# Gnn-to-gnn units of a four-layer graph network: fetched tiles' scores and the side products placed earlier and pinned, the diagonal's sum formed in the next unit

## The chip, the cores and the metric

The kernel runs on one core of a Trainium2 chip. The time is microseconds on the device for one execution of the whole program; the figure used is the median of several runs. The five engines of the core are TensorE (PE, with its weight loads shown apart as PEld), VectorE (DVE), ScalarE (ACT), GpSimd (POOL) and SyncE (SP), and each works through its own instructions in order. Transfers between the chip's memory and the on-chip buffers are issued by SP and POOL.

## The reference

There are 64 graphs of 256 nodes with 256 features each, all with the same sparse symmetric adjacency matrix. Layers 0, 1 and 3 are alike ("gnn" layers), layer 2 is an attention layer. Everything is in float32.

```python
# layers 0, 1 and 3; h is (64, 256, 256)
pre_u = einsum('bud,dk->buk', h, W1[:d]); pre_v = einsum('bvd,dk->bvk', h, W1[d:])
hidden = relu(pre_u[:, :, None, :] + pre_v[:, None, :, :] + b1)
S = sigmoid(einsum('buvk,ko->buvo', hidden, W2)[..., 0] + b2[0])
a_t = einsum('buv,bud->bvd', S * adj, h)
m_t = einsum('uv,bud->bvd', adj, h) * h
z = beta1*h + beta2*(a_t @ Wa + ba) + beta3*(m_t @ Wm + bm)
# layer 2
feats = data @ W1.T; f1 = feats @ W2 + b2[0]
coefs = softmax(leaky_relu(f1[:, :, None] + f1[:, None, :]) + adj)
out = coefs @ feats + bias2 + data
```

Since S is multiplied by adj, only scores of pairs that are joined by an edge are needed. The kernel computes the scores of edges and of the diagonal alone.

## The kernel before

**Edges as tiles.** The edges are sorted once, at the start, into 16 blocks of up to 128 edges, a few left over ("left", one score column), and the diagonal. One block is a tile of 128 edges for two graphs: a row holds pre_u of the edge's one end plus pre_v (with b1) of the other. Eight blocks (`FAST`) are *made* by PE: a 0/1 matrix `pick` times rows gathered in `pre`, which ACT copies out of pu and pv (rows_u L754, rows_v L763); the product is `ga` (L700). The other eight (`FETCHED`) are *fetched*: pu and pv are written by SP to tables in the chip's memory (L635, "tableu", "tablev"), and POOL gathers rows of them by index (L745), first from the u table, then from the v table with an add onto the first. `FETCHES` is the order of these 18 gathers (16 for tiles, two for `left`, written -1); each gather is kept behind the one before it. The first six are issued when half of the tables is written, the rest at the start of the next unit.

**Scores.** For each tile and graph DVE computes relu, times W2, and the sum over the row in one instruction (`rated`, L664, two per tile by `both`), into a column of `raw`. `rated_all` makes the sigmoid of a stretch of columns: ACT computes `val` (L684, L685), and DVE multiplies it into the edge values (`rm`, L692). The columns come in two stretches. EARLY holds left, the diagonal and the blocks of row half m = 0; LATE holds the blocks of m = 1. Diagonal scores come from `own` = pu + pv of the same node, which `before` adds on DVE from PSUM (L639). `early` puts the left-over edges and the diagonal into the score matrix `sa`: PE computes the `sides` (L774), DVE adds the diagonal (L778). `spread` puts the other edges in: PE multiplies rm by `gu` (L790, first the half m = 0, then m = 1), and DVE adds the result to sa (L792).

**Units.** Graphs go in pairs, in two streams, a and b. A *unit* is one call of `beside(heavy, light)`: `heavy` is the scores of one stream's pair in one layer, `light` is everything else for the other stream's pair, from the end of one layer to the start of the next:

- `after`: spread (L790), then `finish`: aT = h times sa (L281 with sa), the products with Wm and Wa (L369, or L355 after layer 3), and the sum hT on DVE (L372);
- in the unit to layer 2 and on, `attention` (L404 to L454);
- `before`: pu and pv of the next layer in four groups (L628), which ACT and DVE take out of PSUM (L629, L630), the tables, and for layer 1 the two `turn`s (transposes, L287); then `mixed`: the products with adj (L281 with adj), two PSUM tiles whose elementwise product (mT) is kept for the next unit (`later`, L795).

Light is a generator that yields after each piece how many made tiles (`p`) and fetched tiles (`f`) of heavy come next; `got` in `before` gives some of these numbers. A scheduler then orders each engine's instructions by priority and its own costs, so an instruction may stand elsewhere than the program puts it, unless `tc.issue_after` holds it behind another.

Six units make a round of four graphs, and there are 16 rounds: two that go from layer 0 to layer 1 (the *first* and *second gnn unit*), then the first and second attention unit, then two that close layer 3 and open layer 0 of the next graphs (the *layer-3 units*). The scores of a unit are used at the start of the next but are computed beside the other stream, so a late score delays L790 of the next unit. PSUM has five buffers `ps` for light work and three `ga` for made tiles.

Of the kernel before, what the change touches and what calls it, by code (L numbers as in the profile page):

```python
# [15 lines left out]
P = 128  # L16
# [16 lines left out]
FAST = [(0, 0, 2), (0, 0, 3)] + [(0, 1, i) for i in range(4)] + [(1, 0, 2), (1, 0, 3)]  # L33
# [4 lines left out]
FETCHES += [(-1, 0), (2, 1), (4, 0), (3, 1), (5, 0), (-1, 1), (6, 0), (4, 1), (7, 0), (5, 1), (6, 1), (7, 1)]  # L38

AHEAD = 6  # L40

# [16 lines left out]
def quarter(q):  # L58
    return slice(q * 64, (q + 1) * 64)

# [18 lines left out]
def adj_seq_kernel(ctx: ExitStack, tc: tile.TileContext, a: dict, out: bass.AP):  # L79
# [15 lines left out]
    mm = nc.tensor.matmul  # L95
# [36 lines left out]
    def z_weights(l):  # L132
        for kept, n, beta in ((wm, "Wm", "beta3"), (wa, "Wa", "beta2")):
            kept[l] = const.tile([P, 2, D], FP, name=l + n)
            nc.sync.dma_start(out=kept[l], in_=a[l + n].rearrange("(c p) e -> p c e", p=P))
            nc.scalar.mul(kept[l], kept[l], sca(l + beta))
        zbias[l] = const.tile([P, 2], FP, name=l + "zbias")
        zb = const.tile([P, 2], FP, name=l + "zb")
        nc.vector.tensor_scalar(zb, vecs[:, VEC[l + "ba"], :], sca(l + "beta2"), None, ALU.mult)
        nc.vector.scalar_tensor_tensor(  # L140
# [5 lines left out]
    for l in GNN:  # L146
        halfb2[l] = const.tile([P, 1], FP, name=l + "halfb2")
        nc.vector.tensor_scalar(halfb2[l], sca(l + "b2"), 0.5, None, ALU.mult)
    twob2 = const.tile([P, 1], FP, name="twob2")
    nc.vector.tensor_scalar(twob2, sca("L2_gnn_b2"), 2.0, None, ALU.mult)  # L150
# [7 lines left out]
    def counts(keep, pool, pc):  # L158
# [3 lines left out]
        nc.vector.tensor_scalar(mask, adj, 0.0, None, ALU.not_equal)  # L162
# [6 lines left out]
        nc.vector.tensor_tensor_scan(upto.rearrange("p s v -> p (s v)"), flat, flat, 0.0, ALU.add, ALU.bypass)  # L169
        past = pool.tile([P, 8], FP, name="past")  # L170
        nc.vector.memset(past, 0.0)
        nc.vector.tensor_copy(past[:, 1:8], upto[:, 0:7, 63])
        deg = pool.tile([P, 8], FP, name="deg")
        nc.vector.tensor_tensor(deg, upto[:, :, 63], past, ALU.subtract)
# [17 lines left out]
        nc.vector.tensor_copy(first, t[:, 0:8])  # L192
        last = keep.tile([P, 8], FP, name="last")
        nc.vector.tensor_tensor(last, first, deg, ALU.add)

        over = pool.tile([P, 8], FP, name="over")
        nc.vector.tensor_scalar(over, t[:, 8:16], -128.0, 0.0, ALU.add, ALU.max)
        begin = keep.tile([P, 9], FP, name="begin")
        nc.vector.memset(begin, 0.0)
        nc.vector.tensor_tensor_scan(begin[:, 1:9], over, over, 0.0, ALU.add, ALU.bypass)  # L200
        t = pc()
        mm(out=t[:, 0:1], lhsT=other, rhs=begin[:, 8:9], start=True, stop=True)
        nc.vector.tensor_scalar(begin, begin, t[:, 0:1], None, ALU.add)
        number = keep.tile([P, 8, 64], FP, name="number")
        shift = pool.tile([P, 8], FP, name="shift")
        nc.vector.tensor_tensor(shift, first, past, ALU.subtract)
        nc.vector.tensor_tensor(number, upto, shift.unsqueeze(2).to_broadcast([P, 8, 64]), ALU.add)
        nc.vector.tensor_tensor(number, number, mask.rearrange("p m (s v) -> p (m s) v", v=64), ALU.mult)
# [3 lines left out]
    with tc.tile_pool(name="pc", bufs=2, space=bass.MemoryType.PSUM) as pc, tc.tile_pool(name="cnt", bufs=1) as cnt:  # L212
# [3 lines left out]
        nc.vector.tensor_scalar(many, end, float(LEFT), None, ALU.is_gt)  # L216
# [11 lines left out]
    def attention_weights(one, psum):  # L228
# [8 lines left out]
        nc.vector.tensor_copy(w2q[:, :, D], t[:, 0:2])  # L237
        for c in range(2):
            nc.vector.tensor_scalar(qb[:, c, :], ones, w2q[:, c, D : D + 1], None, ALU.mult)

    def last_bias(one):
# [3 lines left out]
        nc.vector.tensor_scalar(zbrow, zbrow, sca(LAST + "beta2"), None, ALU.mult)  # L245
        nc.vector.scalar_tensor_tensor(zbrow, bmrow, sca(LAST + "beta3"), zbrow, ALU.mult, ALU.add)
# [19 lines left out]
    def stages(pools):  # L266
# [16 lines left out]
        def flip(o, src):  # L283

            for m in range(2):
                for c in range(2):
                    nc.tensor.transpose(o[:, m, blk(c)], src[:, c, blk(m)], ident)  # L287
# [22 lines left out]
        def mixed(st, l, later=None):  # L310

            st["mT"] = mT = one.tile([P, 2, 2, N], FP, tag="mT" + st["side"], name="mT")
            for g in range(2):
# [3 lines left out]
                if later is None:  # L317
                    nc.vector.tensor_tensor(*times)
# [4 lines left out]
        def kept(st, l):  # L323

            hb = one.tile([P, 2, 2, N], FP, tag="hb", name="hb")
            for i in range(2):
                if l == LAST:
                    for m in range(2):
                        nc.vector.scalar_tensor_tensor(
                            hb[:, i, m, :], st["h"][i][:, m, :], sca(l + "beta1"), zbrow, ALU.mult, ALU.add  # L330
                        )
                else:
                    nc.scalar.activation(  # L333
# [4 lines left out]
        def finish(st, l):  # L338

            sa, mT = st["sa"], st["mT"]  # L340
            few_scores = l == GNN[1]
            hb = kept(st, l)
            aT = one.tile([P, 2, 2, N], FP, tag="aT", name="aT")
            for g in range(2):
                t = psum()
                product(t, st["h"][g], sa[:, :, g, :])
                nc.scalar.copy(aT[:, :, g, :], t)
                yield 0 if few_scores else 1
            if l == LAST:
                for g in range(2):  # L350
                    z = psum()
                    for m in range(2):
# [4 lines left out]
                        yield m * (1 + g), 1  # L357
                    o = h_tile(st, g)
                    nc.vector.tensor_tensor(o, hb[:, g], z, ALU.add)
# [606 lines left out]
```

## Time and profile before

| | us |
|---|---:|
| runs shown, median (lowest to highest) | 3519.05 (3515.6 to 3520.39) |
| profiled execution, its time | 3512.57 |
| its span, first to last instruction | 3510.1 |
| PE busy in it | 3447.8 |
| DVE / POOL / ACT busy | 2610.0 / 2230.7 / 1598.8 |
| mean granted TensorE clock | 0.993 |

One round, from the timeline of PE (each unit from its first L790 to the next unit's):

| unit | median us over the rounds |
|---|---:|
| first gnn, second gnn | 32.3, 33.05 |
| first attention, second attention | 43.3, 42.55 |
| first layer-3, second layer-3 | 30.9, 31.5 |

The page gives shares of busy time by engine, the span in 40 slices, the chain of waits that ended last, and groups of instructions by line. A float32 matmul shows as two records. A record of PE lasts longer than its share of the engine, since matmuls overlap: for the time that PE needs, read the distance from one start to the next. The waits view lists an engine's idle time by what ended it. A row of a timeline has the start, the time from first start to last end, the engine, line, operation, tiles and number of records, and in brackets the idle time before it with what ended it.

### The profile page before, as it was taken

The numbers are of one execution on the slowest core, as the hardware profiler recorded it, in microseconds if no ns is written. First come the engines' busy times: TensorE is split into PE (matmuls) and PEld (weight loads), VectorE is DVE, ScalarE is ACT, GpSimd is POOL, SyncE is SP. The second block draws the span as 40 slices with busy tenths as digits, with TensorE's granted clock in tenths as the row PEclk, the third lists the DMA queues.
The fourth block names the chain that finished last, engine by engine and source line by source line (L and its number), as shares of the span: only waits on it lengthen the run. The fifth ranks groups of instructions, "written<-read, shape, count | busy, mean of one in ns | idle before, by whom it ended". The sixth has DMA issues, their size and how long they took to land.

```text
span 3510.1 us, 48385 instructions
## 1 busy us (share of the span) xinstructions
PE 3447.8 (98%) x14328; PEld 2108.7 (60%) x14328; DVE 2610.0 (74%) x10584; ACT 1598.8 (46%) x2929; POOL 2230.7 (64%) x1754
## 2 busy tenths in 40 slices
PE   6999999999999999999999999999999999999998
PEld 3566565656656566565666656656565665656655
DVE  5778686777777777777777777768677777777776
ACT  2454444444444444544444444444444444445452
POOL 3757667575666757667576675766757566675764
PEclk7999999999999999999999999999999999999999
DMA  5768777686777868778687786877768687786865
GB/s 149 168 151 189 155 184 165 163 180 153 186 156 174 177 143 193 158 175 182 142 195 158 181 170 155 188 155 185 163 165 178 149 188 154 179 181 148 192 148 114
DMA packets 274733, 587.25 MB, mean 167 GB/s; under 512 B 37024, under 2 KB 54304, under 8 KB 274464
## 3 DMA queue, kind: packets, MB, share of 16 engines
q0 software_dynamic: 190464, 427.93, 61.4%
q1 hardware_dynamic: 82416, 154.96, 12.6%
q8 instruction: 116, 1.90, 0.2%
q10 hardware_dynamic: 1584, 1.20, 0.1%
q14 instruction: 153, 1.25, 0.1%
HBM read 466.51 MB, written 117.44 MB: 166 GB/s over the span
## 4 chain that ended last, share of the span: by engine, by line
PE 67%; DVE 4%; POOL 3%; DMA 3%; issue 2%; ACT 0%; POOLq 0%; DVEq 0%
PE ps L281 13%; PE ga L700 13%; PE ps L628 12%; PE ps L369 8%; PE ps L355 5%; PE ps L790 4%; PE ps L451 3%; PE ps L410 3%; POOL fetched L745 2%; PE ps L287 2%; DMA fetched<-tablev,ids_v 2%; PE ps L774 2%; DVE junk L664 2%; PE ps L404 1%; DVE rm L692 1%
## 5 line engine op out<-in xcount | busy, mean ns | idle before, releaser
L745 POOL DMA_INDIRECT fetched<-tablev,ids_v x768 | 1211.3, 1577 | 351.0 <-issue 237.4
L745 POOL DMA_INDIRECT fetched<-tableu,ids_u x768 | 766.8, 998 | 806.1 <-DMA tableu<-pu 576.1
L700 PE MATMUL ga<-pre,pick 128*128 128x512 f32 x1536 | 775.2, 604 | 10.5 <-DVE junk L664 7.9
L628 PE MATMUL ps<-L_gnn_w,hT 128*128 128x512 f32 x1536 | 695.4, 596 | 5.7 <-DMA hT<-in_xT_dram 5.7
L664 DVE SCALAR_TENSOR_TENSOR junk<-ga,L_gnn_w2row 128x256 f32<-128x256 f32 x1536 | 583.5, 420 | 119.8 <-PE ga L700 114.8
L664 DVE SCALAR_TENSOR_TENSOR junk<-fetched,L_gnn_w2row 128x256 f32<-128x256 f32 x1536 | 596.1, 419 | 32.6 <-DMA fetched<-tablev,ids_v 32.1
L763 ACT COPY pre<-pv 64x512 f32<-64x512 f32 x768 | 473.4, 616 | 107.1 <-DVE pv L630 76.3
L628 PEld LDWEIGHTS ps<-L_gnn_w,hT 128*128 128x128 f32 x1536 | 285.1, 191 | 334.6 <-issue 311.2
L754 ACT COPY pre<-pu 64x1024 f32<-64x1024 f32 x384 | 392.9, 1039 | 3.8
L700 PEld LDWEIGHTS ga<-pre,pick 128*128 128x128 f32 x1536 | 274.9, 191 | 163.6 <-issue 111.9
L372 DVE TENSOR_TENSOR hT<-hb,ps 128x512 f32<-128x512 f32 x128 | 88.0, 688 | 379.0 <-PE ps L369 379.0
L281 PE MATMUL ps<-adj,h 128*128 128x256 f32 x1536 | 361.0, 387 | 6.6 <-DVE own L639 4.7
L281 PE MATMUL ps<-sa,h 128*128 128x256 f32 x1536 | 363.7, 382 | 3.0 <-DVE sa L792 2.6
L281 PEld LDWEIGHTS ps<-sa,h 128*128 128x128 f32 x1536 | 288.9, 190 | 119.3 <-issue 47.3
L629 ACT COPY pu<-ps 128x256 f32<-128x256 f32 x384 | 142.2, 370 | 467.6 <-PE ps L628 449.1
L281 PEld LDWEIGHTS ps<-adj,h 128*128 128x128 f32 x1536 | 284.0, 190 | 77.0 <-issue 34.3
L692 DVE TENSOR_TENSOR rm<-gva,val 128x256 f32<-128x256 f32 x768 | 277.4, 420 | 37.9 <-ACT val L685 27.7
L333 ACT ACTIVATE hb<-hT,L_gnn_zbias,scas 128x512 f32<-128x512 f32 x128 | 97.4, 807 | 450.4 <-DVE hT L372 363.7
L790 PEld LDWEIGHTS ps<-rm,gu 128*64 128x64 f32 x3072 | 175.0, 137 | 123.1 <-PE ps L281 59.1
L369 PE MATMUL ps<-mT,L_gnn_Wm 128*128 128x512 f32 x512 | 240.6, 592 | 0.0
L369 PE MATMUL ps<-aT,L_gnn_Wa 128*128 128x512 f32 x512 | 240.6, 592 | 0.0
L790 PE MATMUL ps<-rm,gu 128*64 128x128 f32 x3072 | 218.5, 280 | 14.6 <-DVE rm L692 12.4
(156 smaller groups left out, 4074.3 us busy)
## 6 DMA issues: line engine op xcount, KB each, us to landing
tableu<-pu SPq DMA_DIRECT2D x192, 256.0 KB
tablev<-pv SPq DMA_DIRECT2D x192, 256.0 KB
hT<-in_xT_dram SPq DMA_DIRECT2D x32, 512.0 KB
h<-in_x_dram SPq DMA_DIRECT2D x64, 256.0 KB
out_dram<-h SPq DMA_DIRECT2D x64, 256.0 KB
fetched<-tableu,ids_u POOLq DMA_INDIRECT x768
fetched<-tablev,ids_v POOLq DMA_INDIRECT x768
L_gnn_w<-in_L_gnn_W_dram SPq DMA_DIRECT2D x6, 256.0 KB
```

The source lines that it names most:

```text
L281: mm(out=o[:, m, :], lhsT=lhs[:, c, blk(m)], rhs=rhs[:, c, :], start=c == 0, stop=c == 1)
L355: mm(out=z[:, m, :], lhsT=y[:, c, g, blk(m)], rhs=w[:, c, :], start=j == 0 and c == 0, stop=j == 1 and c == 1)
L369: mm(out=z, lhsT=w[:, c, blk(m)], rhs=y[:, c], start=j == 0 and c == 0, stop=j == 1 and c == 1)
L628: mm(out=t, lhsT=hT[:, c, g, blk(m)], rhs=w1[l][:, c], start=c == 0, stop=c == 1)
L629: nc.scalar.copy(pu[:, m, g, :], t[:, 0, :])
L664: nc.vector.scalar_tensor_tensor(junk, t, 0.0, w2row[l], ALU.max, ALU.mult, accum_out=raw[:, i : i + 1])
L692: nc.vector.tensor_tensor(rm[:, k, ms, g, :], gva[:, k, ms, :], val[:, i : i + 4].unsqueeze(2).to_broadcast([P, 4, 64]), ALU.mult)
L700: mm(out=t, lhsT=pick[:, k, 4 * m + i, :], rhs=pre[:, n], start=True, stop=True)
L745: this = nc.gpsimd.indirect_dma_start(out=to, out_offset=None, in_=rows, in_offset=bass.IndirectOffsetOnAxis(ap=ids, axis=0), compute_op=( ...
L754: nc.scalar.copy(st["pre"][h, f : f + n], st["pu"][h, m].rearrange("p g d -> p (g d)").unsqueeze(1).to_broadcast([64, n, 2 * D]),)
L763: nc.scalar.copy(st["pre"][halves[1 - k], n], st["pv"][halves[i % 2], i // 2].rearrange("p g d -> p (g d)"))
L790: mm(out=t[h, :, quarter(i)], lhsT=gu[:, k, 4 * m + i, :], rhs=rm[:, k, 4 * m + i], start=True, stop=True)
```

## The change

The units of the two gnn-to-gnn transitions (`placed`) get an order of their own, and some orders change for all units.

- A wrapper (`Noting`) remembers each engine's last instruction. In placed units the made tiles' matmuls, the scores of fetched tiles, left and diagonal, and the first ACT step of `rated_all` are held behind the instruction that the program issued last on that engine (`behind`).
- Light after layer 0 yields fetched tiles from the first piece of `finish` on (`STEPS`), so that EARLY stands ahead of `before`, and `early` is a step of its own ahead of tile 4. EARLY waits for the first four made tiles only; for that `FAST` has the blocks of m = 0 first, and the copies into `pre` follow that order.
- In layer 1, `own` is no longer added in `before`: the unit that computes the scores adds it, from pu and pv, one instruction of 512 columns for each half, and in placed units the diagonal's scores stand ahead of fetched tiles 0 and 1. In the other units they stand with the second and third made tile.
- In `FETCHES` left's v gather goes ahead of tile 5's u gather.

Calls by `nc.vector`, `nc.scalar` and `nc.tensor` become calls by the wrapper everywhere; that is cut here.

```diff
-FAST = [(0, 0, 2), (0, 0, 3)] + [(0, 1, i) for i in range(4)] + [(1, 0, 2), (1, 0, 3)]
+FAST = [(k, 0, i) for k in range(2) for i in (2, 3)] + [(0, 1, i) for i in range(4)]
-FETCHES += [(-1, 0), (2, 1), (4, 0), (3, 1), (5, 0), (-1, 1), (6, 0), ...
+FETCHES += [(-1, 0), (2, 1), (4, 0), (3, 1), (-1, 1), (5, 0), (6, 0), ...
+STEPS = {
+    GNN[0]: [(1, 1), (1, 1), (0, 1), (1, 0), (0, 1), (2, 1)],
+    GNN[1]: [0, 0, 0, 0, 0, 1],
+    LAST: [1, 1, (0, 1), (1, 1), (0, 1), (2, 1)],
+}
+    def behind(engine):
+        return tc.issue_after(engine.last.ins)
...
-                yield 0 if few_scores else 1
+                yield STEPS[l][g]
...
-            got = {LAST: (1, 0, 1, 1), GNN[1]: (1, 1, 1, 1), GNN[0]: (0, 0, 2, 1)}[l]
+            got = {LAST: (1, 0, 1, 1), GNN[1]: (0, 1, 1, 1), GNN[0]: (0, 0, 2, 1)}[l]
-            own = one.tile([P, 2, 2, D], FP, tag="own", name="own")
+            if l != GNN[1]:
+                st["own"] = one.tile([P, 2, 2, D], FP, tag="own", name="own")
...
-                nc.vector.tensor_tensor(own[:, m, g, :], t[:, 0, :], pv[:, m, g, :], ALU.add)
+                if l != GNN[1]:
+                    vector.tensor_tensor(st["own"][:, m, g, :], t[:, 0, :], pv[:, m, g, :], ALU.add)
...
-                    rows_v(st, 2 - 2 * m, 2, 0)
+                    rows_v(st, 4 - 4 * m, 2, 0)
...
                     st["turn"](0)
-                    yield 1
+                    yield 0, 1
                     st["turn"](1)
-                    yield 0, 1
+                    yield 0
...
-        def scores(st, l):
+        def scores(st, l, placed):
+            stay = behind if placed else lambda engine: nullcontext()
...
+                with stay(scalar):
+                    scalar.activation(val[:, cols], raw[:, cols], AF.Tanh, bias=halfb2[l], scale=0.5)
...
+            def itself(m):
+                with stay(vector):
+                    if l == GNN[1]:
+                        vector.tensor_tensor(*(flat(t)[:, m] for t in (own, st["pu"], st["pv"])), ALU.add)
+                    both(own[:, m], DIAGONAL + 2 * m, DIAGONAL + 2 * m + 1)
...
+                    with stay(tensor):
+                        mm(out=t, lhsT=pick[:, k, 4 * m + i, :], rhs=pre[:, n], start=True, stop=True)
...
-                            rows_u(st, 2 * n + 2, 2, n // 2, 1 - n // 2)
-                            if n:
-                                rows_v(st, 2 * n + 2, 2, n // 2)
-                    if n < 2:
-                        both(own[:, n], DIAGONAL + 2 * n, DIAGONAL + 2 * n + 1)
+                            rows_u(st, 2 * n + 2, 2, *FAST[2 * n + 2][:2])
+                            if n != 1:
+                                rows_v(st, 2 * n + 2, 2, FAST[2 * n + 2][0])
+                    if n in (1, 2) and not placed:
+                        itself(n - 1)
...
                     if f == FIRST:
-                        for _ in made:
-                            yield
-                        rated(left, REST)
+                        if placed:
+                            while len(count) < 4:
+                                next(made)
+                        else:
+                            for _ in made:
+                                yield
+                        with stay(vector):
+                            rated(left, REST)
                         rated_all(EARLY, 0)
                         yield
-                    tile_scores(fetched[f], *block)
-                    if f == FIRST + 1:
+                        if placed:
+                            early(st)
+                            yield
+                    if f < 2 and placed:
+                        itself(f)
+                    with stay(vector):
+                        tile_scores(fetched[f], *block)
+                    if f == FIRST + 1 and not placed:
                         early(st)
                     yield
...
-                yield [after(st, GNN[0]), before(st, GNN[1])], (st, GNN[1])
+                yield [after(st, GNN[0]), before(st, GNN[1])], (st, GNN[1]), True
```

## The prediction

> **What bounds the kernel now.** I read the engine shares first, then who TensorE (PE) waits for, then the timeline of PE and VectorE (DVE) across a unit that goes from layer 0 to layer 1.
>
> ```profile
> PE 3447.8 (98%) x14328; PEld 2108.7 (60%) x14328; DVE 2610.0 (74%) x10584; ACT 1598.8 (46%) x2929; POOL 2230.7 (64%) x1754
> ...
> PEclk7999999999999999999999999999999999999999
> ```
>
> PE is busy nearly all the time at full clock, so it sets the time. Busy is not yet packed, though: 512-column records last 592 to 604 ns each in the groups, but in the chain of waits sixteen L369 records take 6.87 us, 429 ns apiece. I therefore count spacing between starts, not busy time. Where nothing waits, 512 columns cost 0.43 us and 256 columns 0.216. Judged so, only some tens of microseconds are waits. PE's waits:
>
> ```profile
> PE ps L790 <- DVE rm L692: 12.4, 10, 6.0
> PE ga L700 <- DVE junk L664: 7.9, 3, 6.8
> ...
> PE ps L281 <- DVE own L639: 4.7, 5, 2.4
> ```
>
> The L700 wait is start-up. The first and third lie in the units of this change. PE where one gnn unit meets the next, then where it meets an attention unit, then where the first gnn unit begins:
>
> ```profile
> 2056.05 1.02 PE L700 MATMUL ga<-pre,pick 128*128 128x512 f32 x2
> 2057.00 1.09 PE L790 MATMUL ps<-rm,gu 128*64 128x128 f32 x16
> 2058.81 1.42 PE L790 MATMUL ps<-rm,gu 128*64 128x128 f32 x16 [0.71 <-DVE rm L692]
> ...
> 2090.07 2.42 PE L790 MATMUL ps<-rm,gu 128*64 128x128 f32 x32
> ```
> ```profile
> 2024.84 1.09 PE L790 MATMUL ps<-rm,gu 128*64 128x128 f32 x16
> 2025.86 1.12 PE L700 MATMUL ga<-pre,pick 128*128 128x512 f32 x2
> 2026.91 1.09 PE L790 MATMUL ps<-rm,gu 128*64 128x128 f32 x16
> 2027.94 1.12 PE L700 MATMUL ga<-pre,pick 128*128 128x512 f32 x2
> ```
>
> The 32 spread records (L790) take 1.70 us from first to last start where nothing waits (the second attention unit, all 16 rounds). In the second gnn unit they take 2.96, in the first attention unit 2.15; the first gnn unit hides its wait behind one L700. What is late is rm, DVE's product of the late scores:
>
> ```profile
> 2051.30 0.43 DVE L664 SCALAR_TENSOR_TENSOR junk<-fetched,L_gnn_w2row 128x256 f32<-128x256 f32 x1 [1.20 <-DMA fetched<-tablev,ids_v]
> ...
> 2051.65 1.46 DVE L692 TENSOR_TENSOR rm<-gva,val 128x256 f32<-128x256 f32 x4
> 2053.03 0.74 DVE L630 TENSOR_TENSOR pv<-ps,L_gnn_b1row 128x256 f32<-128x256 f32 x2
> 2053.69 0.74 DVE L639 TENSOR_TENSOR own<-ps,pv 128x256 f32<-128x256 f32 x2
> 2054.35 1.64 DVE L778 SCALAR_TENSOR_TENSOR sa<-diag,val,ps 128x256 f32<-128x256 f32 x4
> ...
> 2057.66 1.43 DVE L692 TENSOR_TENSOR rm<-gva,val 128x256 f32<-128x256 f32 x4 [0.63 <-ACT val L685]
> ```
>
> The last gather lands at about 2053.2, but 4.3 us of other DVE work stands between 2051.65 and the last three scores, which end near 2057.0; then val, and rm only at 2057.66. Order on DVE, not data, makes it late.
>
> **What the Trainium skill says.** "Perfetto Trace Analysis", Identifying the Most-Contended Engine: matmul busy share is no measure of headroom because matmuls are pipelined. The trace agrees (592 against 429 ns). The same page, DMA Instruction — SWDGE (GPSIMD): a gather's slice ends when its descriptors are written, and the data move later. The trace agrees: a v gather is 1.55 us on POOL, and the one issued at 2045.39 is 5.81 us of DMA in the chain; so I reckon a v gather as landing some 5.2 us after its issue. The same page, Optimization Strategy: the same gap repeating on the engine that should be saturated can mean too few buffers for the next tile. That fits the L281 waits on own, which hold a PSUM buffer, but not L790, whose data are missing.
>
> **The change, part by part.** S is the start of L790 in a gnn unit; the order comes from the built program, durations from rows of before.
>
> 1. *Second gnn unit, late scores.* In the new order DVE does the early rm (1.4) and sa (1.6) before tile 4, and own is not there. For the first gnn unit: the second L628 pair ends at S+28.2, its pu copy (0.37) and pv (0.42) bring DVE to S+29.1; tiles 6 and 7 landed at S+26.4 and 28.4; four scores at 0.345 end at S+30.5; val takes 0.6; rm starts at S+31.2. PE's second half started 1.15 us after rm in the excerpt (2058.81 less 2057.66), so at S+32.35 it is free to run, and PE reaches it near S+33.5. The wait goes, with 1.1 us spare: 2.96 - 1.70 = 1.26 in ten of 16 rounds, 0 to 0.82 in the others: **-15.6 us**.
> 2. *First attention unit.* The same in the second gnn unit, with 0.5 us spare because its gathers start later (5 below): 2.15 - 1.70 = 0.45 in 15 rounds and 1.26 in one: **-8.1**. The small waits of sa,h on sa just after it: -1.2.
> 3. *own out of `before` in layer 1.* The adds that free PSUM late go: L281's waits on own by spacing of starts, **-6.7** (idle alone 4.7). DVE does 64 adds of 512 (0.684, L795's row) for 128 of 256 (0.419): 10 us less, all beside PE, worth nothing further.
> 4. *Pinned L700.* In the first gnn unit L790 becomes one block; L700 no longer stands between its halves. Changes L700 to L790 fall from 126 to 110. A split costs 0.34 (4.06 us against 3.72 for the same records), but it covered a wait: the late rm of the layer-3 unit before starts at 2025.21, S+0.37, and that unit keeps its order. The second half can start at S+0.37+1.15 = 1.52, the block takes 2.67, and with the usual 2.02 to the first sa,h this is 4.69 against 4.06: +0.63 in 16 rounds, **+10.1**.
> 5. *Moved steps and their queues.* One L700 more stands ahead of the first L628 pair (+0.86 after +0.63, less waits gone), so pu reaches SP's table DMA about 1.3 us later; POOL, which already waited 2.8 us for it at 2051.64, starts the next unit's 18 gathers so much later. These take 29 us of 32: they land in time, but half the slack of step 2 goes. On POOL `left`'s v gather goes before one u gather (0.98 plus 0.3): left lands 1.3 us sooner, and the u gather 1.9 later with 4 us in hand. No DMA is added.
> 6. *Waits behind pinned scores.* hT (L372) now stands on DVE behind tiles 1, 2 and 3. Tile 3 lands at S+14.4, and hT's second half is not fed by PE until S+17.5. val stands on ACT ahead of the pu copies; it is ready near S+20, and the first L628 group ends at S+20.9. sides take two of five PSUM buffers early; sa frees them by S+25.6, L628 needs one at S+26.5. All zero while gathers land within 2 us of today's times; 1 us per us beyond.
> 7. L774 sooner: PE changes shape as often as before; zero. FAST order, ACT's copies: the same number, and the rows for the third L700 are ready at S+2.5 for its use at S+3.7; zero. Units not placed: own's scores one L700 later, with none behind them waiting; zero. Start and end of the run: 2 us either way.
>
> The trace doesn't show PE in the pinned order. From below, step 4 may cost nothing (rm a little earlier, the split saved: -5.4); from above, a gather later by its own spread (1 us) takes back steps 1 and 2 in part. I take the values above.
>
> Sum: -15.6 - 8.1 - 1.2 - 6.7 + 10.1 = **-21.5 us**. The profiled execution took 3512.57 us with a span of 3510.1; the median of runs is 3519.05, 6.5 longer, and I take the difference over unchanged: 3519.05 - 21.5 = 3497.5.
>
> **Rivals.** (a) *The gathers become the bound.* Step 5's later table eats the slack, the first attention unit keeps its 0.45 or gets 1 us, and step 1 comes back by half: +8 and -8 for -15.6, net about -4 with steps 3 and 4: 3515, no change. For it: DMA is 81% busy in the gnn units and POOL's sequence fills 29 of 32 us. Against it: tile 7 lands over 4 us ahead of its use. (b) *Slower:* DVE blocks on a gather in front of hT (L372) in the second gnn unit. Slack there is 2.0 us (tile 3 at S+14.75, needed by S+16.75, since PE comes sooner). Beyond that L628 waits us for us; all of the gain is lost when tile 3 is 3.4 us later than today in each round (1.4 times 16), and 4 us give +10: 3529. Against it: nine gathers in ten land within 1 us of the median. (c) *It doesn't place as said:* the built order shows that it does; but if the second gnn unit's stall has another cause (tile 7 itself), steps 1 and 2 are void: +10.1 - 6.7 = 3522.
>
> **How the numbers follow.** 0.2%, about what a measurement here can tell from no change, is 7 us. The sum's case (-8 to -33): 0.77, and more by a free step 4 and fewer stray stalls: 0.04; (a) 0.06 and (c) 0.03, both no change; (b) 0.10. Faster 0.81, same 0.09, slower 0.10. The likeliest case alone spans 3486 to 3511; for eight in ten I reach to part of (a): 3484 to 3514.
>
> **What would show it.** Right: the 32 L790 records of the second gnn and first attention units take about 1.7 us, rm in PE's waits moves to the first gnn unit (near 2.7 us there, some 0.6 to 1 us per round), own vanishes from L281's waits, own<-ps,pv falls to 256 and DVE's busy time by some 10 us. Wrong: L628 or L774 waiting for hT, ro or pu; DVE's waits on fetched ahead of hT; a first gnn unit over 33 us.

## The result, and the profile after

| | us |
|---|---:|
| after, median of 5 runs (lowest to highest) | 3497.66 (3496.77 to 3504.9) |
| before, median of 5 runs beside it | 3519.05 (3515.6 to 3520.84) |
| ratio, 95% interval | 0.9947 (0.9933 to 0.9962) |
| profiled execution after, its time; its span | 3497.66; 3496.0 |

The forecast was 3497.5. Between the two profiled executions the change is smaller, 14.9 us (3512.57 to 3497.66). Run again later, beside other runs of the kernel before, the same changed kernel stood at 0.991 (0.9896 to 0.9925). So the forecast's total hit the first measurement and is small for the second; what separates the two is taken up below.

The wrapper issues nearly everything in the changed kernel, so its profile gives the wrapper's line, L76; rows are told apart by tiles (ps<-rm,gu is L790, ga<-pre,pick L700, ps<-adj,h and ps<-sa,h the two kinds of L281, junk<-fetched the gathered scores). The engine shares:

```profile
PE 3430.6 (98%) x14328; PEld 2112.8 (60%) x14328; DVE 2621.2 (75%) x10520; ACT 1617.1 (46%) x2929; POOL 2244.3 (64%) x1754
```

PE is busy 17.2 us less for the same instructions; DVE is busy 11.2 us more with 64 instructions fewer. TensorE's part of the waits view (us in total, times, longest):

```profile
PE ps L76 <- DVE rm L76: 17.4, 18, 6.3
...
PE ps L76 <- DVE sa L76: 7.3, 8, 1.9
...
PE ps L76 <- DVE own L76: 0.6, 1, 0.6
```

The wait on own is down to one, outside the rounds. The wait on rm is longer than before (17.4 for 12.4; the longest single wait of each, 6.3 and 6.0, is in the run's last unit; the prediction read all 12.4 as lying in the units of the change, but summed by distances of starts). PE's timeline shows where a first gnn unit begins, and then where the second begins:

```profile
2010.51 1.02 PE L76 MATMUL ga<-pre,pick 128*128 128x512 f32 x2
2011.46 1.09 PE L76 MATMUL ps<-rm,gu 128*64 128x128 f32 x16
2014.04 1.42 PE L76 MATMUL ps<-rm,gu 128*64 128x128 f32 x16 [1.49 <-DVE rm L76]
...
2044.23 1.02 PE L76 MATMUL ga<-pre,pick 128*128 128x512 f32 x2
2045.18 1.97 PE L76 MATMUL ps<-rm,gu 128*64 128x128 f32 x32
2047.08 1.98 PE L76 MATMUL ga<-pre,pick 128*128 128x512 f32 x4
```

In the second gnn unit the 32 records are now one piece without a wait, in all 16 rounds. In the first they break after 16, with nothing between: the wait on rm has moved there. (This round is one of two in which a gather came late too: its 32 records take 3.73 us, where the median is 2.70.) DVE's timeline on the way to that second gnn unit:

```profile
2036.52 1.66 DVE L76 SCALAR_TENSOR_TENSOR sa<-diag,val,ps 128x256 f32<-128x256 f32 x4 [0.23 <-PE ps L76]
...
2041.38 0.42 DVE L76 TENSOR_TENSOR pv<-ps,L_gnn_b1row 128x256 f32<-128x256 f32 x1 [0.61 <-ACT pu L76]
2041.73 0.41 DVE L76 SCALAR_TENSOR_TENSOR junk<-fetched,L_gnn_w2row 128x256 f32<-128x256 f32 x1
...
2043.84 1.43 DVE L76 TENSOR_TENSOR rm<-gva,val 128x256 f32<-128x256 f32 x4 [0.63 <-issue]
```

sa is done before the late scores, and only four scores stand between the last pv and rm. rm starts 1.34 us before L790 does; before, it started 0.66 us after it.

Summed by unit over the profiled rounds, from the distances between PE's starts (us; "again" is the changed kernel's second profiled execution, span 3486.9):

| unit (number of units) | before | after | again |
|---|---:|---:|---:|
| first gnn (16) | 523.7 | 525.2 | 524.3 |
| second gnn (16) | 524.5 | 508.9 | 507.7 |
| first attention (16) | 695.6 | 687.1 | 684.5 |
| second attention (16) | 682.7 | 689.2 | 680.8 |
| first layer-3 (15) | 463.6 | 465.8 | 463.5 |
| second layer-3 (15) | 473.2 | 473.4 | 474.8 |

The differences add up to -13.7 and -27.7. Ahead of its first unit the second execution took 3.3 us more than the kernel before.

### The profile page after: what moved, and what is told of

Read it like the earlier page. It is cut to its first block, busy times and chain, and to the rows that moved or that the text cites. A ratio compares the mean times of both kernels' runs of the same rounds, so it can differ in the third digit from the quotient of the medians.

```text
span 3496.0 us, 48605 instructions
## 1 busy us (share of the span) xinstructions
PE 3430.6 (98%) x14328; PEld 2112.8 (60%) x14328; DVE 2621.2 (75%) x10520; ACT 1617.1 (46%) x2929; POOL 2244.3 (64%) x1754
## 4 chain that ended last, share of the span: by engine, by line
PE 87%; DVE 5%; issue 2%; DMA 2%; POOL 2%; ACT 1%; ACTq 0%; POOLq 0%; DVEq 0%
PE ps L76 70%; PE ga L76 17%; DVE junk L76 2%; POOL fetched L803 2%; DMA fetched<-tablev,ids_v 2%; DVE rm L76 1%; DVE sa L76 1%; DVE own L76 0%; DMA fetched<-tableu,ids_u 0%; DVE mT L76 0%; ACT val L76 0%; POOL left L803 0%; DVE pv L76 0%; DMA h<-in_x_dram 0%; DMA L_gnn_b1row<-in_rows_dram 0%
## 5 line engine op out<-in xcount | busy, mean ns | idle before, releaser
L803 POOL DMA_INDIRECT fetched<-tableu,ids_u x768 | 777.1, 1012 | 782.9 <-DMA tableu<-pu 552.3
L76 PE MATMUL ga<-pre,pick 128*128 128x512 f32 x1536 | 771.2, 603 | 8.4 <-DVE junk L76 6.1
L76 PE MATMUL ps<-L_gnn_w,hT 128*128 128x512 f32 x1536 | 696.9, 597 | 5.7 <-DVE L_gnn_zb L76 5.7
L76 DVE SCALAR_TENSOR_TENSOR junk<-ga,L_gnn_w2row 128x256 f32<-128x256 f32 x1536 | 583.7, 419 | 103.5 <-PE ga L76 87.3
L76 DVE SCALAR_TENSOR_TENSOR junk<-fetched,L_gnn_w2row 128x256 f32<-128x256 f32 x1536 | 595.4, 418 | 47.2 <-DMA fetched<-tablev,ids_v 45.7
L76 ACT COPY pre<-pv 64x512 f32<-64x512 f32 x768 | 473.4, 616 | 66.8 <-DVE pv L76 42.1
L76 PEld LDWEIGHTS ps<-L_gnn_w,hT 128*128 128x128 f32 x1536 | 285.7, 191 | 335.5 <-issue 308.3
L76 ACT COPY pre<-pu 64x1024 f32<-64x1024 f32 x384 | 391.9, 1044 | 7.3
L76 PEld LDWEIGHTS ga<-pre,pick 128*128 128x128 f32 x1536 | 278.3, 190 | 180.2 <-issue 126.1
L76 PE MATMUL ps<-sa,h 128*128 128x256 f32 x1536 | 363.9, 382 | 7.6 <-DVE sa L76 7.3
L76 PEld LDWEIGHTS ps<-sa,h 128*128 128x128 f32 x1536 | 291.9, 191 | 121.1 <-issue 60.6
L76 ACT COPY pu<-ps 128x256 f32<-128x256 f32 x384 | 142.8, 372 | 477.4 <-PE ps L76 464.3
L76 PE MATMUL ps<-adj,h 128*128 128x256 f32 x1536 | 354.0, 383 | 1.4 <-issue 1.4
L76 PEld LDWEIGHTS ps<-adj,h 128*128 128x128 f32 x1536 | 286.6, 190 | 73.1 <-issue 31.5
L76 ACT ACTIVATE hb<-hT,L_gnn_zbias,scas 128x512 f32<-128x512 f32 x128 | 97.4, 807 | 478.0 <-DVE hT L76 382.6
L76 DVE TENSOR_TENSOR hT<-hb,ps 128x512 f32<-128x512 f32 x128 | 87.9, 687 | 277.6 <-PE ps L76 261.6
L76 DVE TENSOR_TENSOR rm<-gva,val 128x256 f32<-128x256 f32 x768 | 276.9, 419 | 23.7 <-ACT val L76 17.1
L76 DVE TENSOR_TENSOR pv<-ps,L_gnn_b1row 128x256 f32<-128x256 f32 x384 | 161.9, 422 | 153.2 <-ACT pu L76 146.4
L76 PEld LDWEIGHTS ps<-rm,gu 128*64 128x64 f32 x3072 | 173.8, 137 | 113.3 <-PE ps L76 52.3
L76 PE MATMUL ps<-mT,L_gnn_Wm 128*128 128x512 f32 x512 | 240.6, 592 | 0.0
L76 PE MATMUL ps<-aT,L_gnn_Wa 128*128 128x512 f32 x512 | 240.6, 592 | 0.0
```

The lines of the kernel that those rows point to most:

```text
L76: self.last = getattr(self.engine, op)(*a, **k)
L803: this = nc.gpsimd.indirect_dma_start(out=to, out_offset=None, in_=rows, in_offset=bass.IndirectOffsetOnAxis(ap=ids, axis=0), compute_op=( ...
```

## The experiments

The theory is that of the prediction: DVE's order, not the data, makes the late rm late; the pins put the early sides and scores ahead; the pinned block of the first gnn unit costs 10 us. The rivals: the gathers' landing decides, or own's move is what gains. The kernels ran in three groups of four, in the order below, each group on one chip, where the median of the kernel before was 3509.75, 3513.57 and 3503.48 us. Kernels are compared within a group first; the expectations of the first group were set against the 3519.05 and 3497.66 of another chip, so some 9 us of each are the chip's (3519.05 less 3509.75). A trace is of one execution, and its time is given where it lies far from the median. "Stretch" is the sum over 16 units from L790's first start to its last; undisturbed it is 27.1 us.

### Own alone

```diff
 # before (L639 only where l != GNN[1]); in the unit that computes the scores:
+                        if l == GNN[1]:
+                            nc.vector.tensor_tensor(half(own, n), half(st["pu"], n), half(st["pv"], n), ALU.add)
```

> The kernel before, with one thing of the change: layer 1's own is no longer added where layer 0's update makes pv, but as two adds of 512 in the next unit. No pins, no moved scores or sides, no moved steps. Theory (VectorE's order makes the late rm late): L281's waits on own go (-6.7 us), and about 0.66 us of adds leaves VectorE's path ahead of the late scores, so the second gnn unit's 32 L790 records take some 2.3 us instead of 2.96 and the first attention unit's some 1.7 to 1.8 instead of 2.15: -6.7 - 10.5 - 5.6 = -22.8, that is 3496 to 3503 us, as much as the whole change and without its pinned block. Rival 1 (the gathers' landing decides): only L281's waits go, 3512. Rival 2 (own's place is worth nothing, the order of scores and sides is all): 3517 to 3520.

Measured: 3495.33 us, ratio 0.9962 (0.9948 to 0.9976), about -13 us where -22.8 was expected, and clear of the second rival's nothing. The traced execution was the fastest of five (3488.96), so its stretches show rather more than the median. The second gnn unit's stretch fell from 42.8 to 36.2 (median 2.31 us, as expected), the first attention unit's from 35.4 to 30.4. What the distances between L281's adj records have beyond their usual 0.216 us fell by 6.2 us in the two gnn units together, of 12.0 in the kernel before. So moving own is worth something when everything else stays, and the data do allow an earlier rm. It does not finish either job.

### Own put back

```diff
-            if l != GNN[1]:
+            if True:
                 st["own"] = one.tile(...)      # and the add behind each pv in before
-                    if l == GNN[1]:
-                        vector.tensor_tensor(*(flat(t)[:, m] for t in (own, st["pu"], st["pv"])), ALU.add)
```

> The changed kernel with layer 1's own put back to where it was (four adds of 256, each behind its pv); pins, scores' and sides' places stay. Theory: L281's waits on own come back (+6.7); own stands ahead of the late scores again, but those have 0.5 to 1.1 us to spare, so the second gnn unit's L790 stretch stays at 1.70: 3502 to 3507 us. Rival (own's move is what the change gains by, as 0.66 us off VectorE's path): back to 3515 to 3520, with the second gnn unit's stretch over 2.3.

Measured: 3483.66 us, ratio 0.9925 (0.9912 to 0.9939). Stretches 27.7 and 29.0 us. That is below both expectations, by 9 us even when the chip's 9 are allowed for. L281's excess in the gnn units stays at zero with own back in its old place, where the theory had +6.7. The waits view has, for own:

```profile
PE ps L76 <- DVE own L76: 0.2, 1, 0.2
```

DVE's timeline of this kernel shows why:

```profile
2038.65 0.42 DVE L76 TENSOR_TENSOR pv<-ps,L_gnn_b1row 128x256 f32<-128x256 f32 x1
2039.11 0.42 DVE L76 TENSOR_TENSOR own<-ps,pv 128x256 f32<-128x256 f32 x1
2039.45 0.41 DVE L76 SCALAR_TENSOR_TENSOR junk<-fetched,L_gnn_w2row 128x256 f32<-128x256 f32 x1
```

Own stands directly behind pv and ahead of tile 6. The prediction's excerpt of before had the first late score, which waited for its gather, and rm ahead of pv and own. With sides and scores placed, own no longer stands behind a wait for data; then it can stay. The placement does by itself what own's move does in part.

### The split, and the pins away

```diff
 # the split: in the first gnn unit, between the halves of L790
+                if m == 0 and l == GNN[0] and st["side"] == "a":
+                    yield 1
-            yield 1 if l == GNN[1] else 2
+            yield 1 if l == GNN[1] or (l == GNN[0] and st["side"] == "a") else 2
 # no pins
-            stay = behind if placed else lambda engine: nullcontext()
+            stay = lambda engine: nullcontext()
```

> The changed kernel, but in the first gnn unit one L700 goes between the two halves of L790 again, as before the change (126 splits instead of 110). Theory (step 4: the late rm of the layer-3 unit is waited for in the open, some 1 us per round, and one L700 of 0.86 us covered it at 0.34 per split): rm's 17.4 us in TensorE's waits fall to about 2, the first gnn unit goes from 32.7 to about 32.1 us: -10, 3486 to 3490 us. Rival (the wait only moves: the second gnn unit and hT follow at the pace of the gathers, so a first gnn unit that is sooner done meets a later gather): 3495 to 3499, with more waits on fetched. Rival 2 (a split costs as much as it hides): 3498 to 3503.

Measured: 3475.71 us, ratio 0.9901 (0.9885 to 0.9917). The first gnn unit takes 32.04 us in every round, 512.7 us in all, 11.6 less than in the changed kernel's second execution. PE at its start:

```profile
2007.93 1.12 PE L76 MATMUL ga<-pre,pick 128*128 128x512 f32 x2
2008.99 1.09 PE L76 MATMUL ps<-rm,gu 128*64 128x128 f32 x16
2010.01 1.12 PE L76 MATMUL ga<-pre,pick 128*128 128x512 f32 x2
2010.97 2.32 PE L76 MATMUL ps<-sa,h 128*128 128x256 f32 x10
```

One L700 stands where PE waited. That is step 4 taken by itself, in the reverse direction. PE's waits on rm are still 12.5 us, for the 2 expected: 6.4 in the run's last unit, the rest mostly in first attention units (stretch 32.6).

> The changed kernel without its pins: the same program text, but the two placed units leave the order of scores and sides on each engine to the scheduler. Its order on VectorE then is early rm, pv, tiles 4 and 5, pv, tile 6, the four sa, tile 7, own, pv, late rm, pv, and on TensorE L790 is split in the first gnn unit. Theory: sa is held until tile 6 has landed (S+26.4), so the sides' PSUM buffers come free at about S+28.5 while L628 wants one at S+26.5: some 2 us of TensorE's wait per placed unit, less 10 for the split: 3520 to 3560 us, slower than the kernel before. Rival (where the scores stand is all, a pin adds nothing): 3487 to 3498.

Measured: 3524.5 us, ratio 1.0039 (1.0025 to 1.0053), slower than before. The second gnn and first attention units have no wait on rm left (stretch 27.1 each); all of the loss is in the first gnn unit, 574.7 us, 50 more than with pins. (The traced execution was the slowest of six, 3535.27; by the medians' ratios the pins are worth 1.3%, some 45 us.) PE's waits, then DVE and PE in one such unit:

```profile
PE ps L76 <- DVE pv L76: 23.1, 16, 4.2
PE ga L76 <- ACT pre L76: 18.0, 17, 1.9
```
```profile
1204.61 0.43 DVE L76 SCALAR_TENSOR_TENSOR junk<-fetched,L_gnn_w2row 128x256 f32<-128x256 f32 x1 [2.87 <-DMA fetched<-tablev,ids_v]
...
1205.30 0.42 DVE L76 TENSOR_TENSOR pv<-ps,L_gnn_b1row 128x256 f32<-128x256 f32 x1
```
```profile
1205.78 5.40 PE L76 MATMUL ps<-L_gnn_w,hT 128*128 128x512 f32 x8 [2.08 <-DVE pv L76]
```

The cause is a neighbour of the one expected. It is pv, not sa, that stands behind a score whose gather has not landed: DVE waits 2.87 us for data, and the PSUM buffer that pv empties reaches PE's L628 2.08 us late. ACT's copies into `pre` are late too. This is the prediction's slower rival (b) in another place: work that PE needs, queued on DVE behind a gather. The pins keep it away.

### The changed kernel again

> The changed kernel itself, unaltered, to have it on one chip with the next ones: its time beside the kernel before varied by chip. Its profile of the prediction had late gathers in six first attention units (5.9 us) and sa late behind TensorE's L790 in six second attention units (about 8 us), which the kernels with own back and with the split did not show. If these are stray (theory), most of them are gone here: ratio to before 0.991 to 0.994, about 3483 to 3490 us where before is 3510, second attention unit 42.55 us in nearly all rounds. If they belong to the changed kernel's order on VectorE (rival), they are here again: ratio 0.994 to 0.996, second attention unit over 43 us on the mean.

Measured: 3482.55 us, ratio 0.991 (0.9896 to 0.9925). The profiled execution was the slowest of four (3488.63). Even so its second attention unit takes 42.55 us in every round, and sa is no longer among PE's waits. What set the first profile apart there was stray, in the sense that the same program runs without it. Late gathers in first attention units are here again, in fewer rounds (stretch 30.7 for 33.1).

### Split and own back; layer 0's own moved; sides back

```diff
 # split and own back: both of the edits above
 # layer 0's own moved too (and so where own is made and added)
-            if l != GNN[1]:
+            if l == LAST:
 # sides, sa and early rm back behind tile 5
-                            early(st)
-                    if f == FIRST + 1 and not placed:
+                    if f == FIRST + 1:
```

> The changed kernel with both: one L700 between L790's halves in the first gnn unit, and layer 1's own back behind each pv. Theory after the first runs (own's place is worth nothing once the scores and sides stand early: with own back TensorE waited for own 0.2 us in all): equal to the split alone, ratio to before 0.989 to 0.991. Rival (own late in the next unit delays its sa; own back is a gain by itself, as the run with own back alone, 0.9925, seemed to show): 0.986 to 0.988, 6 us or more below the split alone.

Measured: 3476.66 us, ratio 0.9889 (0.9875 to 0.9904). The interval overlaps both expectations. In the trace the first gnn unit is 513.2 us and the stretches are 29.6 and 32.3 us, no better than with the split alone (27.7 and 32.6): own's place shows no value.

> The changed kernel, and layer 0's own moved to the next unit as well, as two adds of 512 (only layer 3's stays in front). Theory: the late rm of the second layer-3 unit comes about 0.66 us sooner, so the first gnn unit's L790 block, 2.7 us, goes to about 2.0: 0.66 in 16 rounds, -10 us against the changed kernel, first gnn unit 32.0 to 32.1. Rival (rm of that unit is late by its gather or by val, not by own's 1.5 us of adds): stretch stays 2.6 to 2.7, -2 to +2 us; or the wait comes back as sa late in the first gnn unit, which now adds own first: sa waits over 1 us, +5.

Measured: 3477.49 us, ratio 0.9903 (0.9886 to 0.992). In nine rounds the first gnn unit's block takes 2.01 to 2.07 us, for 2.67 to 2.73, and the unit some 32.0 for 32.7, as expected. In seven the block took 2.2 to 4.6 us, so the sum gained little (522.7 us for 524.3); in six of these seven DVE had waited 0.4 to 1.8 us for a gather among its late scores. So own's adds do stand on the path of the late rm of the second layer-3 unit. The time is 5 us below the changed kernel's, for the 10 expected, and the two intervals overlap.

> The changed kernel with sides, sa and early rm (early) back behind tile 5 in the two placed units, as in the kernel before; tiles' scores stay pinned where the change put them. VectorE's order is then tile 4, pv, tile 5, the four sa, pv, tiles 6 and 7, late rm. Theory: tile 5 lands by about S+22.5, so sa ends by S+26.5 as TensorE's L628 wants the PSUM buffer, and the late scores stay ahead: -1 to +5 us against the changed kernel, second gnn unit's stretch 1.70 to 1.9. Rival (early sides are what makes the late scores soon, since 3.1 us of sa and rm stand ahead of tile 4 otherwise): second gnn unit's stretch 2.3 to 3 again, +10 to +20 us.

Measured: 3482.16 us, ratio 0.9912 (0.9898 to 0.9927): the same as the changed kernel (3482.55). Stretches 27.1 and 28.0 us. Early sides are worth nothing by themselves; with the scores pinned, sa stands ahead of tiles 6 and 7 either way, and that is enough.

### The table sooner, both, all, and the gathers' order

```diff
 # table sooner: one L700 from ahead of the first L628 pair to behind it
-    GNN[0]: [(1, 1), (1, 1), (0, 1), (1, 0), (0, 1), (2, 1)],
+    GNN[0]: [(1, 1), (1, 1), (0, 1), (1, 0), (0, 1), (1, 1)],
-                yield 0, got[(m, g)]
+                yield int(l == GNN[1] and (m, g) == (0, 1)), got[(m, g)]
 # gathers' order of before
-... (3, 1), (-1, 1), (5, 0), (6, 0), ...
+... (3, 1), (5, 0), (-1, 1), (6, 0), ...
```

> The split kernel (one L700 between L790's halves in the first gnn unit), and in the two placed units one L700 that stood ahead of the first L628 pair now stands behind it, so pu's copy and the table's DMA leave 0.86 us sooner and the next unit's gathers can start that much earlier. Theory (step 5: the late gathers that TensorE met in some first attention units come of the table that leaves later): the waits on rm in first attention units, 3.8 to 6.9 us by run, fall by half or more; -2 to -4 us against the split alone, ratio to before 0.988 to 0.9895. Rival (the late gathers are spread of the DMA itself, whenever they start): the same 3 to 7 us in other rounds, 0 +- 2 us, ratio 0.989 to 0.991.

Measured: 3495.52 us, ratio 0.9977 (0.997 to 0.9985), against both expectations. (The traced execution, 3500.78, was near the slowest of 22.) The part that was tested came out: the first attention unit's stretch is 27.1 us, with no late gather in any round (32.6 with the split alone). The gathers did start sooner: the first of those that this unit's rm needs was issued 5.20 us ahead of the second gnn unit's L790 (median), for 4.35 with the split alone. But its waits on sa are large:

```profile
PE ps L76 <- DVE sa L76: 21.4, 28, 2.0
```
```profile
3405.76 0.69 DVE L76 TENSOR_TENSOR sa<-sa,ps 128x512 f32<-128x512 f32 x1 [0.91 <-PE ps L76]
3408.68 0.69 DVE L76 TENSOR_TENSOR sa<-sa,ps 128x512 f32<-128x512 f32 x1 [2.23 <-PE ps L76]
```
```profile
3403.97 1.97 PE L76 MATMUL ps<-rm,gu 128*64 128x128 f32 x32
...
3406.83 0.59 PE L76 MATMUL ps<-sa,h 128*128 128x256 f32 x2
3409.42 3.06 PE L76 MATMUL ps<-sa,h 128*128 128x256 f32 x7 [2.00 <-DVE sa L76]
```

L790's records are over at 3405.94. DVE's second add into sa, which needs them alone, starts 2.7 us later, released by PE, and sa,h waits for it. In the trace's semaphore events PE's updates come some 0.7 us apart from 3404.98 to 3408.65; in the same place of the changed kernel's second execution they come 0.22 us apart. So PE's matmuls, or their signals, came late here although the records look the same.

> The split kernel with layer 0's own moved to the next unit as well. Theory: the first gnn unit has nothing left to gain (its wait is covered by the L700), stays at 32.04 us; the second layer-3 unit's late rm comes sooner too (31.53 to 31.25, as with own moved and no split): -4 us against the split alone, ratio to before 0.988 to 0.9895. Rival (the two gains add, so own's move reaches more than rm): -8 to -10, ratio 0.9865 to 0.988. Rival 2 (less spare time before layer 0's own in the next unit, sa late): 0.991 and above.

Measured: 3483.29 us, ratio 0.995 (0.9935 to 0.9964). The second layer-3 unit went to its expected 31.25 us (median). The second attention unit took 695.3 us, 14.5 above undisturbed, with sa late again. The ratio is in the range of rival 2, but not by its reason: that was an sa made late by layer 0's own, which is used in the gnn units, and the run just above lost the same without moving it.

> The split, layer 0's own in the next unit and the table's L700 behind the L628 pair, all three. Theory: the sum of what the parts give against the changed kernel, -10 for the split, -4 for own, -2 to -4 for the table: ratio to before 0.987 to 0.989, the shortest of all. Rival (what is left is the gathers' spread, no order on an engine reaches it): no shorter than the split alone, 0.989 to 0.991.

Measured: 3491.15 us, ratio 0.9966 (0.9958 to 0.9974). First attention stretch 27.1 us again, sa late in both attention units (their sa,h records take 13.4 us more than undisturbed). Neither the theory's sum nor the rival's reason: the gathers were reached, and another wait took the gain. Its 22 runs, one build on one chip, go from 3480.7 to 3500.79 us.

> The changed kernel with the order of gathers of the kernel before: tile 5's u gather ahead of left's v gather on GpSimd's queue. Theory (step 5: the u gather has 4 us in hand, left's 1.3 us aren't needed): -2 to +2 us against the changed kernel, ratio to before 0.990 to 0.993. Rival (tile 3 to 5 stand ahead of hT and pv on VectorE now, so a u gather that comes 1.9 us sooner shows): -4 to -6. Rival 2 (left is needed sooner now): +4 to +10, with TensorE waiting on ro's L774.

Measured: 3482.21 us, ratio 0.9946 (0.9931 to 0.996). Beside the changed kernel's 3482.55 us on another chip this is nothing; the ratio is larger because the kernel before was 10 us faster on this chip. First gnn unit 523.0 us and stretches 27.1 and 29.2: the gathers' order has no visible effect.

## Why the prediction was right, and where it was not

**The direction and its main reason stand.** Step 1 said -15.6 us from the second gnn unit. The stretch fell from 42.8 to 27.2, which is 15.6. The order on DVE was the cause: own alone brought 6.6 of it with the same gathers. The rest goes, by elimination, to the tiles' scores placed sooner (`STEPS` and the order of the made tiles): the stretch stayed between 27.1 and 27.7 with own back, with the early sides back and without the pins, each taken away alone. No run moved the scores alone, so this part is argued and not shown.

**Step 4, the pinned block, stands.** It forecast a block of 2.67 us, and 2.67 to 2.73 is what undisturbed rounds show. From the first L790 to the first sa,h the first gnn units took 77.7 us in sum, for 66.0 before: the block cost 11.7 us, for the 10.1 forecast, and over 2 of it are the two rounds with a late gather. The unit itself grew by 1.5 us alone, since L281's excess there (10.4 us) went. The split gave 11.6 back.

**Step 2 was right in sum and wrong in its terms.** The first attention unit fell by 8.5 us, for -8.1 and -1.2. But the term -8.1 for its L790 measured -2.3 in the first execution and -4.7 in the second. The failing number is the "0.5 us spare": six rounds of the first execution took 2.0 to 3.5 us for the block, and in each of them DVE had waited for a gather. In one of them, DVE and then PE:

```profile
584.82 0.42 DVE L76 SCALAR_TENSOR_TENSOR junk<-fetched,L_gnn_w2row 128x256 f32<-128x256 f32 x1 [2.30 <-DMA fetched<-tablev,ids_v]
...
585.52 0.69 DVE L76 TENSOR_TENSOR own<-pu,pv 128x512 f32<-128x512 f32 x1
586.23 1.43 DVE L76 TENSOR_TENSOR rm<-gva,val 128x256 f32<-128x256 f32 x4
```
```profile
585.21 1.09 PE L76 MATMUL ps<-rm,gu 128*64 128x128 f32 x16
587.47 1.33 PE L76 MATMUL ps<-rm,gu 128*64 128x128 f32 x16 [1.16 <-DVE rm L76]
```

DVE has nothing left but this tile and waits 2.30 us for it; rm is late by the data, which is rival (a) in some rounds. By the updates of the gathers' semaphores the last gather landed 5.0 us ahead of this unit's first L790 in the kernel before (median), and 2.3 after, once only 0.5: the gathers start later, and L790 comes sooner. Rival (a) was dismissed because tile 7 lands "over 4 us ahead of its use"; that was so before and not after. The table experiments confirm the link that step 5 drew: with the table sooner the last gather landed 3.8 us ahead (3.1 at least), and no first attention unit had a late one. The term -1.2 for the sa,h records measured -5.9 (58.0 us from the first to the last, now 52.1). Three of their distances had been 0.28 to 0.32 us for 0.216 in the median round (3.51 us from first to last, now 3.24), which the list of waits does not show, and these went too. The two errors cancelled by luck.

**Step 3 had the effect, but not its size and only half of its cause.** L281's excess in the gnn units fell by 12.0 us in all, for 6.7 forecast; the distances over 0.45 us alone make the 6.7, and the smaller ones went too. The prediction put it down to own's move. Own put back did not bring it back; the placement suffices, and own's move alone reaches half. The prediction also read these waits through the Trainium skill ("Perfetto Trace Analysis", Optimization Strategy), by which a gap that repeats can mean too few buffers. No buffer was added in any run here: the excess went from 12.0 us to zero by the order on DVE that frees the buffers.

**What steps 5 to 7 put at zero stands where it was tested**: the gathers' order and sides' place changed nothing measurable. Step 5's later table is the one that cost, in step 2's slack.

**A term that was missing.** The forecast had zero for the second attention unit and the layer-3 units. The first execution lost 6.5 and 2.4 us there, mostly with sa late; the second gained 1.9 in the one and lost 1.5 in the other. In the second attention and first layer-3 units the sa,h records took 10.6 us more than undisturbed in the first execution; without that its -13.7 would be near -24. The agreement of 3497.5 with 3497.66 also rests on the 6.5 us by which the median before lay above its profiled execution. The prediction carried them over, but the profiled execution after is itself the median: 14.9 of the measured 21.4 us are in the traces, and 6.5 are that difference. So the agreement is better than the sum's terms deserve, and partly luck.

**The expected sign that failed:** DVE's busy time did not fall by 10 us, it rose by 11.2. The instructions' own durations, added up, fell from 3362.8 to 3344.8 us. But busy time counts overlap once, and instructions back to back overlap; 245 fewer neighbours overlap in the new order (9275 for 9520). Busy time of DVE is thus no sum of durations, and the prediction treated it as one.

**What stays open:** why PE's completions came 0.7 us apart in some L790 blocks. Late sa of this kind held PE in the changed kernel's first execution but not in its second, in the three combined kernels of the third group, once in the kernel with the old order of gathers there, and in a few rounds of the kernel before. It goes with the chip or the moment more than with the kernel. In the eight profiled executions of the first two groups DVE's second add into sa never started over 1.03 us after L790's last record. In the six others it started over 1.2 us after it in 7 of 96 blocks (before; in some of them DVE itself was busy), 10 (after), and 40, 17, 29 and 7 (the third group in its order). Within the third group the kernels differ, and so do the runs of one kernel, so build and moment are not separated. The times of the third group therefore don't say what the table's place or layer 0's own is worth. For the same reason no version is shown to beat the changed kernel everywhere: the split did by its trace, but the changed kernel did not run on that chip, and the intervals of their ratios (0.9901 and 0.991) overlap; the split with layer 0's own, 3483.29, did not beat the old order of gathers, 3482.21, beside it.

## What to carry to other kernels

On an engine that works in order, list what stands ahead of the late instruction and ask of each whether it waits for data that come later; a copy out of PSUM left behind a gather cost about 50 us here, more than the whole change gave, and the pins kept it away. Where a wait can't be removed, put a piece of the bottleneck engine's own work into it: one L700 hid 11.6 us. When spare time is smaller than the spread of a transfer's landing, price the slack by that spread and not by its median, and from the order after the change, where everything else has moved as well.

## What the runs showed of the hardware

After some waits of about 2 us PE's clock was halved for a while. In the timeline above, where the last row ends with its window, the seven distances between sa,h records from 3410.14 to 3413.13 are 0.427 us, where 0.216 is usual; the windows view of this kernel has (columns from the left: window, length, busy time of PE, PEld, DVE, ACT and POOL with their instructions, granted clock, DMA share, GB/s):

```profile
3408.00:3409.00 1.00, 0.00 (x0) 0.00 (x0) 0.32 (x1) 0.00 (x0) 0.73 (x1) 1.00 0.84 215
3409.00:3410.00 1.00, 0.58 (x2) 0.56 (x3) 1.00 (x3) 0.00 (x0) 0.96 (x1) 0.88 0.63 131
```

The trace's clock record has half speed for 3.4 us from 3409.75. Such a stall costs about 1.7 us beyond itself, some eight sa,h records at twice their distance: in the changed kernel's first execution the one second attention unit with it took 46.4 us for 42.55, with 2.1 us of wait. Not every wait did it: the same kernel had a distance of 1.91 us between two sa,h records at 808.4 with no change of clock, and the kernel without pins one of 3.05 us between two matmuls at 337.8. What decides it is not shown.
